# Attention scores from float32r halves on two row tiles, with the maxima of two heads taken in one reduce

## The chip, the cores and the metric

The kernel runs on one core of one Trainium2 chip. Its time is what the device took for one execution, in microseconds (us). Of several runs the median is given; one further execution was profiled, and all rows of engines, waits and chains below come from that one.

## The reference

One sequence of 2048 tokens with 256 features goes through six stages, each added to the residual x after a layer norm: feed-forward f0, attention 0, feed-forward f1 (the same weights as f0), feed-forward f2 (another kind), attention 1, feed-forward f3 (as f2). Cut to the two attentions, which the change concerns:

```python
qkv = x @ W_qkv                       # layer 1: x @ Wq.T + bq, and so on, then rope on q and k
q, k, v = heads(qkv)                  # 16 heads of 16 features
attn = q @ k.T / 4 + alibi + causal   # layer 1: no alibi; alibi = slope[head] * (j - i)
attn = softmax(attn)
y = attn @ v
x = x + y @ W_o                       # layer 1: + bo
```

Everything is float32. In layer 1 the biases of q and k are large, so the scores need more than the precision of one bf16 product.

## The kernel before

The sequence is cut into four chunks of 512 columns (`CH`), and features lie on the partitions. The feed-forwards go chunk by chunk (`feed_forwards`, line 457): gate and up products in float32r pairs (f0, f1: `gate_up0`, line 295, each activation split into a top part and a rest) or in float32 (f2, f3: `gate_up`, line 271), an activation, a projection back (`tail0`, `tail1`). In f0 the weights are quantized beside the first chunk (`quantize`, line 130), from raw tiles that SP loads. The attentions are one function (`attention`, line 513), called for each layer.

**Scores from parts.** `prep_qk` (line 544) makes q and k of one chunk, splits each value into three bf16 parts (cast on ACT, differences on DVE and POOL) and writes them to DRAM so that six products of parts (`Q_PARTS`, `K_PARTS`) lie under each other. `load` (line 651) reads, for a group `n` of four heads and a chunk, tiles `qs[n]` and `ks[n, kc]`: 96 rows of six products by 16 features, and below them rows for the negated row maximum (three bf16 parts) and, in layer 0, for the alibi bias. One bf16 matmul over these 105 rows (99 in layer 1) gives the scores of one head for 128 x 512 places, with the maximum already subtracted once its rows are there.

**Two passes.** The score is taken twice. `mx_unit` (line 702) computes it with the queries on the partitions (tile `pq`, one PSUM bank for each head) and reduces it on DVE to the maximum of each row (line 721). When all maxima of a group are there, `mx_end` and `mx_turn` negate, split and transpose them and put them into the rows of `qs[n]` by DMA. Then `st_pair` (line 764) computes the transposed scores of two heads (tile `pst`, two banks), `exp_pair` takes their exponential on ACT into `pT` (one instruction for two heads, line 792; of the pairs in slots without a unit every third lies in two single banks, line 795), and `av_part` (line 798) multiplies by v: four heads at once on four column tiles of 32 columns, all into one bank `pav`, in float32. A column of ones in v gives the sum of the exponentials; `divide` (line 818) transposes and divides.

**Diagonal blocks.** Where keys and queries are of the same chunk, a further bf16 matmul of 128 columns adds a causal mask for each head (lines 718 and 780).

**Order.** PE, ACT, DVE and POOL run in the order in which the program is written; SP's DMAs are ordered by the framework. The main loop (line 985) goes over 160 slots in each layer: slot (n, kb) is a group of four heads (16 of them, four for each chunk of queries) and a block of 128 keys. A slot takes two `st_pair`s, the units of maxima planned for it (`maxima`, one in most slots, two in 12, none in 19, for a group that comes later), two `exp_pair`s, the pav of an earlier slot (`sums`), and then one step of the preparation of the next chunk, of the output projection, of a layer norm or of `mx_turn`. In a slot with a unit the four heads of the unit stand two by two behind the two `st_pair`s. If the slot is the first, the second or one of the last five of its group, pav is taken in two pieces, one behind each pair; otherwise in one, at the end.

**PSUM.** There are three pools for the whole kernel (lines 55 to 57): two tiles of two banks (`pair`), three of one bank (`one`) and one of one bank (`acc`). `pst` lies in `pair`; `pq` lies in `one`, as do all smaller products in attention (`pp`, `pv`, `pwo`, `ptm`, layer norms); `pav` is `acc`.

Of the kernel before, what the change touches and what calls it, by code (L numbers as in the profile page):

```python
# [12 lines left out]
F32 = mybir.dt.float32  # L13
BF16 = mybir.dt.bfloat16
# [24 lines left out]
Q_PARTS = (0, 0, 1, 1, 0, 2)  # L39
K_PARTS = (0, 1, 0, 1, 2, 0)  # L40
TERMS = len(Q_PARTS)
RM = TERMS * D
ROWS = {0: RM + 9, 1: RM + 3}
# [4 lines left out]
def macaron_kernel(ctx: ExitStack, tc: tile.TileContext, a, out):  # L48
# [6 lines left out]
    ps2 = ctx.enter_context(tc.tile_pool(name="ps2", bufs=2, space=PSUM))  # L55
    ps3 = ctx.enter_context(tc.tile_pool(name="ps3", bufs=3, space=PSUM))
    ps1 = ctx.enter_context(tc.tile_pool(name="ps1", bufs=1, space=PSUM))

    def ps_pair(name):
        return ps2.tile([P, 2, CH], F32, tag="pair", name=name)  # L60

    def ps_one(name):
        return ps3.tile([P, CH], F32, tag="one", name=name)

    def ps_acc(name):
        return ps1.tile([P, CH], F32, tag="acc", name=name)
# [22 lines left out]
    ident = cpool.tile([P, P], F32, name="ident")  # L89
    make_identity(nc, ident)  # L90
    ident_b = cpool.tile([P, P], BF16, name="ident_b")
    nc.vector.tensor_copy(ident_b, ident)

    mask_qk = cpool.tile([P, P], BF16, name="mask_qk")
    mask_kq = cpool.tile([P, P], BF16, name="mask_kq")
    for mask, step, row in ((mask_qk, -1, 1), (mask_kq, 1, -1)):
        nc.gpsimd.memset(mask, 0.0)
        nc.gpsimd.affine_select(
            out=mask, in_=mask, compare_op=ALU.is_ge, fill=MASK, base=0, pattern=[[step, P]],
            channel_multiplier=row,  # L100
        )

    half_m = cpool.tile([P, P], BF16, name="half_m")
    nc.vector.memset(half_m, 0.0)
    nc.vector.memset(half_m[0:64, 0:64], 1.0)
    nc.vector.memset(half_m[64:128, 64:128], 1.0)
# [3 lines left out]
    ones_m = cpool.tile([P, P], F32, name="ones_m")  # L110
    nc.vector.memset(ones_m, 1.0)
# [6 lines left out]
    lpool = ctx.enter_context(tc.tile_pool(name="ln", bufs=1))  # L118
# [9 lines left out]
    qp = raw_scope.enter_context(tc.tile_pool(name="quant", bufs=3, side="right"))  # L128
# [220 lines left out]
    def tail0(c, ss, parts, hp, own, name):  # L349
# [23 lines left out]
        nc.tensor.matmul(pss, lhsT=ones_m, rhs=ss, start=True, stop=True)  # L373
        r = root(pss, eps_rms, 4.0 / F, f"rms_{name}")
# [138 lines left out]
    def attention(layer, before, following):  # L513
# [9 lines left out]
        with ExitStack() as st:  # L523
# [5 lines left out]
                for w in "kq"  # L529
                for c in range(NCH)  # L530
            }

            def values(pool, c):
# [692 lines left out]
```

## Time and profile before

| | |
|---|---|
| median of 3 runs | 1827.77 us (1824.9 to 1831.12) |
| profiled execution: its time | 1831.77 us |
| profiled execution: its span, from the first to the last instruction | 1830.0 us |
| mean granted TensorE clock | 0.974 |
| attention of layer 0, by its stages | 212 to 756 us |
| attention of layer 1, by its stages | 1085 to 1647 us |
| HBM read, written | 59.51 MB, 27.26 MB |

In the profile PE is TensorE's matmuls, PEld its weight loads, DVE is VectorE, ACT ScalarE, POOL GpSimd and SP the engine that issues most DMAs. A row of the timeline gives start, length, engine, line, operation, what it writes and reads, the shape and the number of instructions joined in it; in brackets stand the idle time of the engine just before it and what ended that. Rows joined run from the start of the first to the end of the last, and ends of matmuls are modelled, so the spacing of starts tells more than the length. A row of stages gives the stretch, its length, and busy time and number of instructions for PE, PEld, DVE, ACT and POOL, then the granted clock, the share of the DMA engines and GB/s.

### The profile page before, as it was taken

The page shows a single profiled execution, that of the slowest core. Times are in us where ns is not written, and L with a number is a line of the kernel's source. Part 1 is how long each engine was busy: PE and PEld are TensorE (multiplying, and loading weights), DVE is VectorE, ACT ScalarE, POOL GpSimd, SP SyncE. Part 2 cuts the span into 40 slices and gives each one's busy share as a digit, 9 for nine tenths or more (in the row PEclk, how much of TensorE's full clock was granted, in tenths as well). Part 3 has the DMA queues.
Part 4 walks back from the last instruction along what each step waited for, and adds up shares of the span by engine and source line. Part 5 has one row for each costly group of instructions (what it writes and reads, how often), then busy time and mean ns, then how long its engine had stood idle before and what let it go on. Part 6 is the DMA issues. An engine that isn't in the chain of part 4 may idle for free.

```text
span 1830.0 us, 26213 instructions
## 1 busy us (share of the span) xinstructions
PE 1648.4 (90%) x10299; PEld 782.5 (43%) x10300; DVE 1314.3 (72%) x2368; ACT 911.8 (50%) x1220; POOL 347.0 (19%) x346
## 2 busy tenths in 40 slices
PE   4498888999999999788899998899999999988999
PEld 2365543444434443366444444334434434433443
DVE  7865687787788884466666677778788888816664
ACT  4365354555565667555423325445565556674221
POOL 3355520200000001265411232122001000012000
PEclk9799899999999999999999999999999999999999
DMA  4003332212211110200000334222122110000000
GB/s 138 2 1 105 114 95 79 72 54 76 93 41 47 30 30 1 78 1 1 13 0 1 103 109 130 66 85 90 48 65 90 46 46 28 11 2 0 12 12 23
DMA packets 50508, 93.06 MB, mean 51 GB/s; under 512 B 5424, under 2 KB 33072, under 8 KB 50128
## 3 DMA queue, kind: packets, MB, share of 16 engines
q1 hardware_dynamic: 49296, 89.28, 15.9%
q10 hardware_dynamic: 1088, 2.10, 0.4%
q8 instruction: 81, 1.33, 0.3%
q14 instruction: 43, 0.35, 0.1%
HBM read 59.51 MB, written 27.26 MB: 47 GB/s over the span
## 4 chain that ended last, share of the span: by engine, by line
PE 62%; DVE 19%; ACT 4%; issue 2%; POOL 2%; DMA 1%; SPq 0%; DVEq 0%; ACTq 0%; POOLq 0%
PE pav L807 14%; PE pst L772 12%; PE pq L710 11%; DVE mx L721 8%; PE pg_f L276 7%; PE po_f L287 5%; PE pg_f L301 2%; PE pwo L848 2%; PE pp_k L557 2%; PE pp_q L557 1%; PE po_f L356 1%; DVE ge_f L408 1%; PE pv L622 1%; PE pst L780 1%; PE pq L718 1%
## 5 line engine op out<-in xcount | busy, mean ns | idle before, releaser
L721 DVE TENSOR_REDUCE mx<-pq 128x1 f32<-128x512 f32 (+3 forms) x1280 | 696.7, 602 | 132.8 <-PE pq L718 65.4
L792 ACT ACTIVATE pT<-pst 128x1024 f32<-128x1024 f32 (+3 forms) x616 | 536.2, 897 | 335.8 <-PE pst L772 170.7
L710 PE MATMUL pq<-k,q 105*128 105x512 bf16 (+7 forms) x1280 | 385.9, 349 | 53.2 <-DVE mx L721 46.4
L772 PE MATMUL pst<-q,k 99*128 99x512 bf16 (+7 forms) x1280 | 356.5, 352 | 10.6 <-ACT pT L792 6.7
L807 PE MATMUL pav<-pT,va 128*32 128x256 f32 (+1 forms) x4608 | 324.7, 377 | 6.2 <-DVE yt L828 5.0
L276 PE MATMUL pg_f<-xn,wgu 128*128 128x512 f32 x512 | 230.5, 602 | 15.0 <-DVE hr_f L314 15.0
L772 PEld LDWEIGHTS <-k 105*128 105x128 bf16 (+1 forms) x1280 | 111.5, 98 | 233.7 <-issue 168.3
L833 POOL TENSOR_TENSOR zt<-yt,rd 128x64 f32<-128x64 f32 x128 | 42.1, 329 | 807.3 <-DVE rd L832 803.0
L807 PEld LDWEIGHTS pav<-pT,va 128*32 128x32 f32 x4608 | 106.3, 108 | 191.5 <-issue 136.8
L710 PEld LDWEIGHTS <-q 105*128 105x128 bf16 (+1 forms) x1280 | 122.9, 98 | 128.9 <-issue 26.5
L313 ACT ACTIVATE sl_f<-pg_f 128x512 f32<-128x512 f32 x128 | 75.9, 593 | 174.7 <-PE pg_f L276 98.3
L276 PEld LDWEIGHTS pg_f<-xn,wgu 128*128 128x128 f32 x512 | 97.4, 192 | 142.8 <-issue 115.1
L301 PE MATMUL pg_f<-xt_f,wgu 128*128 128x512 f32 x256 | 101.0, 478 | 37.8 <-DVE sl_f L314 20.9
L287 PE MATMUL po_f<-h_f,wd 128*128 128x512 f32 x256 | 112.6, 593 | 1.4 <-DVE h_f L436 1.4
L718 PE MATMUL pq<-mask_qk,ident_b 128*128 128x128 bf16 x512 | 105.4, 222 | 0.0
L780 PE MATMUL pst<-mask_kq,ident_b 128*128 128x128 bf16 x512 | 103.1, 221 | 0.0
L334 POOL TENSOR_TENSOR ss_f<-ss_f,sq_f 128x512 f32<-128x512 f32 x56 | 85.2, 1521 | 88.8 <-ACT sq_f L333 88.2
L314 DVE TENSOR_TENSOR hr_f<-sl_f,pg_f 128x512 f32<-128x512 f32 x64 | 43.7, 683 | 69.1 <-ACT sl_f L313 68.8
L828 DVE STREAM_TRANSPOSE yt<-pav 128x128 f32<-128x128 f32 x128 | 39.8, 311 | 71.1 <-PE pav L807 71.1
L301 PE MATMUL pg_f<-xr_f,wgu 128*128 128x512 f32 x256 | 86.0, 419 | 1.5 <-DVE xr_f L231 1.5
L314 DVE TENSOR_TENSOR sl_f<-sl_f,pg_f 128x512 f32<-128x512 f32 x64 | 43.7, 682 | 60.2 <-ACT sl_f L313 59.8
L301 PEld LDWEIGHTS pg_f<-xt_f,wgu 128*128 128x128 f32 x256 | 51.7, 208 | 80.8 <-DVE sl_f L314 27.5
(134 smaller groups left out, 1755.1 us busy)
## 6 DMA issues: line engine op xcount, KB each, us to landing
k<-dk SPq DMA_DIRECT2D x80, 384.0 KB
dk<-p_k SPq DMA_DIRECT2D x48, 256.0 KB
dq<-p_q SPq DMA_DIRECT2D x48, 256.0 KB
q<-dq SPq DMA_DIRECT2D x32, 384.0 KB
x<-in_xT ACTq DMA_DIRECT2D x4, 512.0 KB
raw<-in_w_gu SPq DMA_DIRECT2D x8, 256.0 KB
wgu<-in_w_gu SPq DMA_DIRECT2D x1, 2048.0 KB
cs_k<-in_cos_sin SPq DMA_DIRECT2D x4, 512.0 KB
```

What stands on the lines that cost most here:

```text
L276: nc.tensor.matmul(pg[:, half, :], lhsT=wgu[:, dc, half * F + f * P : half * F + (f + 1) * P], rhs=xn[:, dc, :], start=dc == 0, stop=dc == ...
L287: nc.tensor.matmul(po, lhsT=w[:, f, dc * P : (dc + 1) * P], rhs=h[:, f, :], start=f == 0, stop=f == FC - 1,)
L301: nc.tensor.matmul(pg[:, half, :], lhsT=wgu0[:, dc, half * F + f * P : half * F + (f + 1) * P], rhs=xp[part][:, dc, :], start=part == 0 an ...
L314: nc.vector.tensor_tensor(to, sl, pg[:, 1, :], ALU.mult)
L334: nc.gpsimd.tensor_tensor(ss, ss, sq, ALU.add)
L710: nc.tensor.matmul(pq, lhsT=qs[n][0:rows, hh, t * P : (t + 1) * P], rhs=ks[n, kc][0:rows, hh, 0:w], start=True, stop=kc < c,)
L718: nc.tensor.matmul(pq[:, w - P : w], lhsT=ident_b, rhs=mask_qk, start=False, stop=True)
L721: nc.vector.tensor_reduce(mxs[n][:, t, hh, kc : kc + 1], pq, AX.X, ALU.max)
L772: nc.tensor.matmul(ps[i][:, lo:CH], lhsT=ks[n, kc][0:rows, hh, t * P : (t + 1) * P], rhs=qs[n][0:rows, hh, lo:CH], start=True, stop=kc < c,)
L780: nc.tensor.matmul(ps[i][:, lo : lo + P], lhsT=ident_b, rhs=mask_kq, start=False, stop=True)
L792: nc.scalar.activation(pT[:, :, lo:CH], pair[:, :, lo:CH], AF.Exp, scale=0.25)
L807: nc.tensor.matmul(acc[hh * SLOT : (hh + 1) * SLOT, a:b], lhsT=va[kc][:, t, v0 : v0 + SLOT], rhs=pTs[hh // 2][:, hh % 2, a:b], start=kb == ...
```

## The change

- **Parts.** q and k are split into two float32r parts instead of three bf16 parts (top, and the rest by one subtraction that writes float32r), and three products are kept instead of six. The 52 rows of a head (48 and 4; layer 1: 50) fit into 64 partitions, so two heads lie under each other, at partitions 0 and 64, and the four heads of a group in two columns. The bytes of the tiles and of the DRAM parts stay; a load is four DMAs instead of two.
- **Scores.** `score` issues the matmuls of two heads one behind the other, one on each row tile of 64 rows, into two banks, and the mask, where there is one, as two halves of 64 rows for each head (`eye`, and masks cut in two). Both passes use it.
- **Maxima.** `pq` is a tile of two banks, and one reduce takes the maxima of two heads. The maxima are split into two float32r parts, and go to `qs[n]` in four DMAs instead of three.
- **PSUM.** During attention the pools are three `pair`, one `one`, one `acc`; outside it they are as before.
- **Slots.** pav is taken in one piece at the end of every slot, exp follows each pair, and no pair lies in single banks.
- **Constants.** The rows of biases go through one load, a cast on DVE and a write to DRAM at the start; the masks are made on POOL after the first layer norm; `ones_m` is dropped; three tags of the quantizer have two buffers instead of three. In the order in which SP issues, the load of wqkv (768 KB) now stands ahead of the raw weights.

```diff
-Q_PARTS = (0, 0, 1, 1, 0, 2)
-K_PARTS = (0, 1, 0, 1, 2, 0)
+Q_PARTS = (0, 0, 1)
+K_PARTS = (0, 1, 0)
 TERMS = len(Q_PARTS)
 RM = TERMS * D
-ROWS = {0: RM + 9, 1: RM + 3}
+ROWS = {0: RM + 4, 1: RM + 2}
+HALF = P // 2
...
+    def halves(t, step, row, compare, fill):
+        nc.gpsimd.memset(t, 0.0)
+        for b in range(2):
+            for j in range(2):
+                at = t[b * HALF : (b + 1) * HALF, j, :]
+                nc.gpsimd.affine_select(
+                    out=at, in_=at, compare_op=compare, fill=fill, base=row * j * HALF,
+                    pattern=[[step, P]], channel_multiplier=row,
+                )
+
+    def make_masks():
+        halves(eye, -1, 1, ALU.not_equal, 1.0)
+        halves(mask_qk, -1, 1, ALU.is_ge, MASK)
+        halves(mask_kq, 1, -1, ALU.is_ge, MASK)
...
                     if layer == 0:
                         nc.scalar.copy(pt[0][:, i, :], pp)
-                        nc.vector.tensor_tensor(dn[:, i, :], pp, pt[0][:, i, :], ALU.subtract)
+                        nc.vector.tensor_tensor(
+                            pt[1][:, i, :], pp, pt[0][:, i, :].bitcast(F32), ALU.subtract
+                        )
...
-                    nc.vector.tensor_tensor(dn, dn, pt[0], ALU.subtract)
+                    nc.vector.tensor_tensor(pt[1], dn, pt[0].bitcast(F32), ALU.subtract)
                 yield
-                nc.scalar.copy(pt[1], dn)
-                nc.gpsimd.tensor_tensor(pt[2], dn, pt[1], ALU.subtract)
-                yield
-                for j in range(3):
+                for j in range(2):
...
                 def stack(to, what, of, extra):
+                    halves = to.bitcast(F32).rearrange("(b r) a t -> b r a t", b=2)
+                    for b in range(2):
+                        u = g % 2 * 4 + 2 * b
+                        nc.sync.dma_start(
+                            out=halves[b, 0:RM],
+                            in_=parts[what, of][g // 2]
+                            .bitcast(F32)
+                            .rearrange("m (d u) t -> (m d) u t", u=HB)[:, u : u + 2, :],
+                        )
+                        nc.sync.dma_start(
+                            out=halves[b, RM:rows], in_=extra[b, 0 : rows - RM].bitcast(F32)
+                        )
...
             pools.insert(0, kv)
+            open_psum(3, 1)
...
-            def mx_unit(n, t, kc, heads):
+            def score(out, lhsT, rhs, mask, at):
+
+                for b in range(2):
+                    nc.tensor.matmul(
+                        out[:, b, :], lhsT=lhsT[b * HALF : b * HALF + rows],
+                        rhs=rhs[b * HALF : b * HALF + rows], start=True, stop=mask is None,
+                    )
+                if mask is not None:
+                    for j in range(2):
+                        for b in range(2):
+                            h = slice(b * HALF, (b + 1) * HALF)
+                            nc.tensor.matmul(
+                                out[:, b, at : at + P], lhsT=eye[h, j, :], rhs=mask[h, j, :],
+                                start=False, stop=j == 1,
+                            )
+
+            def mx_unit(n, t, kc, pair):
...
-                for hh in heads:
-                    pq = ps_one(f"pq{layer}_{n}_{t}_{kc}_{hh}")[:, 0:w]
...
-                    nc.vector.tensor_reduce(mxs[n][:, t, hh, kc : kc + 1], pq, AX.X, ALU.max)
+                pq = ps_pair(f"pq{layer}_{n}_{t}_{kc}_{pair}")[:, :, 0:w]
+                score(
+                    pq,
+                    qs[n][:, pair, t * P : (t + 1) * P],
+                    ks[n, kc][:, pair, 0:w],
+                    mask_qk if kc == c else None,
+                    w - P,
+                )
+                nc.vector.tensor_reduce(mxs[n][:, t, pair::2, kc], pq, AX.X, ALU.max)
...
-                for m in range(3):
-                    nc.sync.dma_start(out=qs[n][RM + m : RM + m + 1, :, :], in_=qx[4 * m : 4 * m + 4, :])
+                for m in range(2):
+                    for b in range(2):
+                        at = b * HALF + RM + m
+                        nc.sync.dma_start(
+                            out=qs[n].bitcast(F32)[at : at + 1, :, :],
+                            in_=qx.bitcast(F32)[4 * m + 2 * b : 4 * m + 2 * b + 2, :],
+                        )
...
-                if units:
-
-
-                    full = 1 < kb < c * T - 1
-                    for hp in (1, 0):
-                        ps = st_pair(n, kb, hp)
-                        mx_next(units[0], (2 - 2 * hp, 3 - 2 * hp))
-                        pTs[hp] = exp_pair(n, kb, hp, ps)
-                        if not full:
-                            sums(i - 2 + (hp == 0), hp)
-                    if full:
-                        sums(i - 1, 1)
-                else:
...
+                for pair in (1, 0):
+                    ps = st_pair(n, kb, pair)
+                    if units:
+                        mx_next(units[0], (pair,))
+                    pTs[pair] = exp_pair(n, kb, pair, ps)
+                sums(i - 1, 1)
...
     load_x(0, nc.scalar)
+    raw = rp.tile([P, CH], F32, tag="raw", name="raw_bias")
+    nc.scalar.dma_start(out=raw, in_=a["bias"])
+    bias = lpool.tile([P, CH], F32R, tag="sd", bufs=2, name="bias")
+    nc.vector.tensor_copy(bias, raw)
+    biases = dram.tile([2, NCH, 2, 4, 2, CH], F32R, name="biases")
+    nc.sync.dma_start(
+        out=biases.bitcast(F32).rearrange("w n b r a t -> (w n b r a) t"), in_=bias.bitcast(F32)
+    )
```

## Prediction

> **What bounds the kernel now.** I read the page first, for the engines and the chain that ended last.
>
> ```profile
> PE 1648.4 (90%) x10299; PEld 782.5 (43%) x10300; DVE 1314.3 (72%) x2368; ACT 911.8 (50%) x1220; POOL 347.0 (19%) x346
> ...
> PE 62%; DVE 19%; ACT 4%; issue 2%; POOL 2%; DMA 1%; SPq 0%; DVEq 0%; ACTq 0%; POOLq 0%
> ```
>
> PE is the chain. The busy times by stage show where the edited lines stand: attention of layer 0 runs from 212 to 756 us, of layer 1 from 1085 to 1647 us.
>
> ```profile
> 572.00:747.00 175.00, 169.60 (x1506) 68.67 (x1505) 119.22 (x227) 118.22 (x143) 9.63 (x20) 1.00 0.08 24
> ```
>
> In the last chunk of layer 0 PE (first figure after the length) is busy 169.6 of 175 us, DVE 119, ACT 118. Third, the timeline of one interior slot with a maxima unit:
>
> ```profile
> 644.83 0.61 PE L772 MATMUL pst<-q,k 105*128 105x512 bf16 x2
> 645.05 0.31 PEld L710 LDWEIGHTS <-q 105*128 105x128 bf16 x2
> 645.27 0.59 PE L710 MATMUL pq<-k,q 105*128 105x512 bf16 x2
> 645.47 1.95 ACT L792 ACTIVATE pT<-pst 128x1024 f32<-128x1024 f32 x2 [0.96 <-PE pst L772]
> 645.49 0.31 PEld L772 LDWEIGHTS <-k 105*128 105x128 bf16 x2
> 645.68 2.49 DVE L721 TENSOR_REDUCE mx<-pq 128x1 f32<-128x512 f32 x4 [0.43 <-PE pq L710]
> 645.70 0.59 PE L772 MATMUL pst<-q,k 105*128 105x512 bf16 x2
> 645.92 0.31 PEld L710 LDWEIGHTS <-q 105*128 105x128 bf16 x2
> 646.13 0.67 PE L710 MATMUL pq<-k,q 105*128 105x512 bf16 x2
> 646.73 0.59 PEld L807 LDWEIGHTS pav<-pT,va 128*32 128x32 f32 x16 [0.50 <-issue]
> 646.74 1.07 PE L807 MATMUL pav<-pT,va 128*32 128x256 f32 x16
> 647.73 0.11 PEld L772 LDWEIGHTS <-k 105*128 105x128 bf16 x2 [0.41 <-issue]
> 647.74 0.39 PE L772 MATMUL pst<-q,k 105*128 105x512 bf16 x1
> ```
>
> A slot is 647.74 - 644.83 = 2.91 us of PE without a hole: eight score matmuls 0.216 apart, then pav. DVE needs 2.49 of it, ACT 1.95. Taking each slot's first pst row, the medians are: interior 2.91 (pav in one piece), 3.02 (in two), 4.63 (two units), 1.97 (no unit); diagonal slots with a unit, by width 512, 384, 256, 128: 3.55, 3.34, 2.60, 2.18.
>
> **The score matmuls.** Two float32r matmuls of 52 (layer 1: 50) rows on two row tiles take the place of two bf16 ones. What float32r costs stands in the feed-forward, where one (L301) waited for DVE (sl_f):
>
> ```profile
> 764.83 0.69 DVE L314 TENSOR_TENSOR sl_f<-sl_f,pg_f 128x512 f32<-128x512 f32 x1 [2.30 <-ACT sl_f L313]
> ...
> 765.57 0.30 PEld L301 LDWEIGHTS pg_f<-xt_f,wgu 128*128 128x128 f32 x2 [2.52 <-DVE sl_f L314]
> 765.57 0.73 PE L301 MATMUL pg_f<-xt_f,wgu 128*128 128x512 f32 x2 [2.10 <-DVE sl_f L314]
> ...
> 765.91 0.42 PEld L301 LDWEIGHTS pg_f<-xr_f,wgu 128*128 128x128 f32 x2
> ```
>
> In a stream they are 0.23 us apart, nearly the bf16 spacing. But here the weight load itself waits, begins 0.052 after DVE ends (765.517), and the first of the two matmuls takes 0.34 instead of 0.23: 0.108 of the load is exposed. The bf16 load at 645.92/646.13 runs ahead of its matmul's wait, and the first pst after pav pays only 0.01. Four-byte loads after pav (pwo, pp) also expose 0.107. Two row tiles at once are in no row; nearest are the column tiles of pav: four matmuls 7 ns apart, whose 16 loads take 0.59 together, like the groups of four, 0.216 apart. So a pair costs between one matmul (0.23) and two (0.46); I take 0.23, the loads likewise side by side.
>
> The page "TensorE: Matmul & The Clock Gate" of the Trainium skill, "Weight-path perf modes", speaks against the change: fast weight load is only for 128 columns that are not FP32. The rows agree for float32r (exposed 0.108 against 0.01), and a sum that loads float32r as fast as bf16 would make the slot 0.2 shorter than mine. Its Part 3 gives 3.07 times for four row tiles, not 4; an estimate from that page puts a pair at about 0.28 instead of 0.23, some 0.1 us more per slot; no run here shows it.
>
> **PSUM is what ends last then.** pst and pq now share three two-bank buffers. A slot uses four: st of pair 1, max of pair 1, st of pair 0, max of pair 0; the fourth takes the buffer of the first and waits for exp of pair 1, in PE's own order, with the whole pav and the next slot's st queued behind it. That closes a loop:
>
> - exp of 1024: 1.025 (L792 by form); release to load: 0.052; exposed load: 0.108
> - max matmuls to first pav: 0.306 (646.429 to 646.735); pav to the next st load: 0.999 (to 647.734)
> - exposed load again 0.108, then pst to exp 0.415 (645.053 to 645.468)
>
> Sum 3.01 us, against 2.91 now. PE would idle some 0.8 us in each slot, and the halved score work lands there. DVE stays below: a reduce costs 281, 417, 549, 682 ns at 128, 256, 384, 512, so 1024 costs 1.217, two 2.43. Merging saves little of DVE: neighbours overlap by 0.08 now (four in 2.49).
>
> By slot kind, per layer (160 slots):
>
> - 51 interior with pav in one piece: 2.91 to 3.01, +5
> - 25 interior with pav in two: one piece now, two tile changes (about 0.09 each way) saved, 3.02 to 3.01, 0; 8 with two units: four reduces, 4 x 1.13, bind as now, 4.6, 0
> - 12 without unit: ACT binds, 2 x 0.925 = 1.85 against 1.97, -1
> - 53 diagonal with one unit: the same loop with exp 1.025, 0.811, 0.593, 0.383, with the slot's own masks (four half-height ones in two steps of 0.06) and the pav of the slot before (0.999, 0.999, 0.78, 0.57): 3.20, 2.88, 2.33, 1.90. 15 x -0.35, 12 x -0.46, 13 x -0.27, 13 x -0.28 = -18
> - 11 other diagonal slots, about -0.3 each: -3
>
> That is -17 per layer, -34 in all.
>
> **What goes the other way.** (1) Other PE work in the slots (pp, pv, pwo, layer norm, ptm; about 45 groups a layer) stands after pav and before the next st, so it lengthens the loop as it lengthens PE now; but the float32r load after it is exposed: 90 x 0.1 = +9. (2) All of it shares one bank instead of three: at 15 places in the order two such groups stand in one slot, and the second waits for an eviction of 0.6 to 1.2 us: +10 (bounds 0 and 18). (3) At the start, SP now issues the 768 KB load of wqkv ahead of the raw weights. The first raw landed at 4.3 us and DVE's chain starts from it, 79% busy in the first slice; at the 380 to 400 KB/us that the DMA moved from 9 to 13 us, 768 KB are 2 us, and the cast of the bias rows on DVE 0.7: +3 (bounds 0 and 5).
>
> **What costs or gains nothing.** The preparation of q and k loses a cast on ACT (1.04 us, 16 times) and a subtraction on POOL (2.16, 16 times). Both stand beside FFN or attention PE work, but at 155.9 the POOL one runs while DVE's hl_f takes 2.52 instead of 0.68 and PE waits 2.01 for it: -3 in all (bounds 0 and -8). DMA bytes are the same; SP issues 671 rows instead of 456, 215 x 0.4 = 86 us of issue spread over 1100, ahead of need by three slots, hidden; if the cover goes, a late k costs about 2 us each time. The q rows of the maxima take four DMAs instead of three: 0.4 behind a 1.7 us landing, at the four places where the chain shows one: within 2 us. POOL's mask selects (12 x 0.29) fall into POOL's idle 23.3 to 25.2 and before x of chunk 1 is needed.
>
> Sum: -34 + 9 + 10 + 3 - 3 = -15. The profiled execution took 1831.8, the median of the runs is 4 less: 1817, and 1813 for the median.
>
> **Rivals.**
>
> - *The loads of the two tiles follow each other.* Then each exposed place of the loop costs 0.108 more: 141 slots with a unit x 0.22 x 2 layers = +61, 1874: slower. For it: each float32r load blocks the next for 0.108 (765.57 to 765.68). Against it: pav's loads of four tiles overlap. It decides as soon as the interior slot is over 3.1 us. Chance 0.16.
> - *The tiles don't run at once* (the change doesn't do what it says): a pair costs 0.46, both pairs in the loop 0.22 more, masks too: 141 x 0.43 x 2 = +121, 1934. Chance 0.07.
> - *PE's clock falls.* The second slice, PE 49% busy, ran at 0.75 clock; the slots would have PE streaming (0.86 + 0.86) / 3.01 = 57%. A slot at half clock adds about 1.5 us; one in ten makes 32 x 1.5 = +48, 1861. Chance 0.1.
> - *The loop is looser*: loads run ahead of the waits as bf16's do, 0.108 twice per slot off: -61, 1752. Against it: the wait of PEld at 765.57. Chance 0.12.
>
> **Numbers.** The forecast case, 1813, has 0.55; its own terms (each slot known to some 0.1 us over 300 slots) make it 1785 to 1845. About 0.3% (5.5 us) is what a measurement of this kernel can tell from no change; within the case I give 0.65 to faster by more, 0.18 to within, 0.17 to slower. Faster: 0.55 x 0.65 + 0.12 = 0.48; within: 0.10; slower: 0.42. The range 1752 to 1880 takes in the looser loop and the serial loads, and leaves out the case of no concurrency and the worse half of a fallen clock.
>
> **What would show it.** Right: interior slots at 3.0 us, PE's idle before the max matmuls of pair 0 put down to ACT (exp), two score matmuls starting within 10 ns; diagonal slots shorter by 0.3; DVE rows of 1.2 us. Wrong: score pairs 0.3 or more apart (serial loads) or 0.45 (no concurrency); PEclk below 9 in the attention slices; interior slots at 2.8 (loads ahead); or waits of PE on DVE instead of ACT, which would make the reduce the bound.

## The result, and the profile after

The changed kernel takes 1953.76 us (median of 4 runs, 1938.03 to 1968.75) against 1829.44 for the kernel before: a ratio of 1.0653, 95% interval 1.0564 to 1.0742. It is slower, and the forecast was 1813. The ratio is that of the mean times of the fast runs (the run of 1968.75 counts as slow and is left out, a fifth run of 1950.65 is taken in), so it is below the quotient of the medians. The profiled execution took 1966.04, the longest of the four that the ratio takes in, at the lowest granted clock of them (0.899; the others 0.904 to 0.920); its span is 1964.1. First the page: the rows of busy time, of the chain, and of the granted clock in 40 slices.

```profile
PE 1645.9 (84%) x11324; PEld 819.9 (42%) x11324; DVE 1288.9 (66%) x1728; ACT 889.3 (45%) x1180; POOL 317.4 (16%) x341
...
PEclk9799757779988899998999996699898799999999
...
PE 54%; ACT 15%; DVE 14%; issue 4%; POOL 2%; DMA 1%; SPq 0%; DVEq 0%; ACTq 0%; POOLq 0%
```

PE is busy as long as before (1645.9 against 1648.4) in a longer span; ACT's share of the chain went from 4% to 15%; and the clock, 9 in most slices before, is at 5 to 7 in the first slices of the first attention (a slice is 49 us) and at 6 in the first two of the second. Cut from the first slot of each attention to its last, the stages read so (length; busy time of PE, PEld, DVE, ACT, POOL; granted clock):

```profile
224.87:823.82 598.95, 504.05 (x4658) 235.72 (x4658) 382.70 (x510) 299.38 (x362) 34.35 (x75) 0.84 0.18 49
1185.77:1772.98 587.21, 488.91 (x4680) 231.70 (x4677) 399.90 (x529) 303.53 (x360) 51.23 (x85) 0.89 0.21 55
```

Before, they took 519.00 and 537.49 us at clocks of 0.99 and 0.98. So 130 of the span's 134 us more are lost here. The start, where I had expected 3 us more, is within the scatter of the runs: attention begins at 224.9 (before 227.9; in the kernels below 222 to 232).

**The interior slot is as forecast.** The same timeline as before, one interior slot with a maxima unit:

```profile
701.40 0.50 PE L741 MATMUL pst<-q,k 52*128 52x512 f32 x2
701.51 0.19 PEld L741 LDWEIGHTS pq<-k,q 52*128 52x128 f32 x2
701.74 0.40 PE L741 MATMUL pq<-k,q 52*128 52x512 f32 x2
701.80 0.19 PEld L741 LDWEIGHTS pst<-q,k 52*128 52x128 f32 x2
701.94 1.94 ACT L828 ACTIVATE pT<-pst 128x1024 f32<-128x1024 f32 x2 [1.11 <-PE pst L741]
701.97 0.39 PE L741 MATMUL pst<-q,k 52*128 52x512 f32 x2
...
703.02 0.50 PE L741 MATMUL pq<-k,q 52*128 52x512 f32 x2 [0.66 <-ACT pT L828]
...
703.45 1.07 PE L840 MATMUL pav<-pT,va 128*32 128x256 f32 x16
...
704.45 0.50 PE L741 MATMUL pst<-q,k 52*128 52x512 f32 x2
```

Two score matmuls share one row (x2): they and their weight loads start 3 or 4 ns apart, and the next pair follows 0.23 later (701.74 to 701.97). The fourth use of the three buffers, pq at 703.02, waits for ACT's exp with pav behind it. The loop: exp and release 701.94 to 703.02, 1.08; to pav 0.43; pav to the next scores 1.00; those to exp 0.54; together 3.05.

**The diagonal slot is not.** One whose unit is 384 wide (the first row is the maxima of pair 1):

```profile
683.31 0.96 DVE L768 TENSOR_REDUCE mx<-pq 128x2 f32<-128x768 f32 x1
...
684.32 0.64 PE L840 MATMUL pav<-pT,va 128*32 128x256 f32 x8
684.43 0.96 DVE L768 TENSOR_REDUCE mx<-pq 128x2 f32<-128x768 f32 x1 [0.16 <-PE pq L749]
685.30 0.30 DVE L861 STREAM_TRANSPOSE yt<-pav 128x128 f32<-128x128 f32 x1
...
685.66 0.64 PE L840 MATMUL pav<-pT,va 128*32 128x256 f32 x8 [0.71 <-DVE yt L861]
```

pav has two parts, and `av_part` calls `divide` between them: yt transposes the finished columns of the same bank. Here the first part ends while DVE is in the second reduce of 0.96; yt starts when that is done, and only after yt the second part of pav. Before, the scores of the other pair stood between the parts. This slot takes 4.23 us where 2.88 was forecast. (0.34 of it is `ptm`, which half of the slots of this width hold, before the change too, and which the 2.88 leaves out.)

**The clock is the third thing.** Three windows of 3.4 us (columns as in the stages above):

```profile
426.40:429.80 3.40, 2.72 (x40) 1.56 (x38) 2.33 (x5) 1.96 (x4) 0.29 (x1) 1.00 0.45 124
429.80:433.20 3.40, 1.98 (x18) 0.81 (x18) 3.19 (x6) 1.77 (x2) 0.29 (x1) 1.00 0.55 131
433.20:436.70 3.50, 3.50 (x22) 1.22 (x22) 3.19 (x3) 1.02 (x1) 0.00 (x0) 0.51 0.00 0
```

After a window with PE busy 1.98 of 3.40 and DVE 3.19, PE runs at half clock. What stands in that window isn't a diagonal slot but the end of an interior slot with two units, and the slot after it:

```profile
430.46 0.74 PE L741 MATMUL pq<-k,q 52*128 52x512 f32 x4
...
431.50 0.50 PE L741 MATMUL pst<-q,k 52*128 52x512 f32 x2 [0.30 <-DVE mx L768]
...
431.80 4.59 DVE L768 TENSOR_REDUCE mx<-pq 128x2 f32<-128x1024 f32 x4
...
433.12 0.71 PE L741 MATMUL pq<-k,q 52*128 52x512 f32 x2 [1.12 <-ACT pT L828]
```

PE issues the second unit's maxima at once (430.46) and goes on. DVE then has four reduces in a row (4.59 us), the second unit's two and the next slot's own. The next scores wait for a buffer from DVE (0.30), the next maxima for exp (1.12). Of the 16 interior slots with two units in both layers 15 have half clock in them or in the slot behind them (2 of 16 before). All stretches of half clock in the trace are multiples of 3.41 us long; in the two attentions there are 21, from 3.4 to 65 us, and they add up to 319 us (25 before). An interior slot that lies in one takes 4.50.

### The profile page after: what moved, and what is told of

The parts are those of the page before. It is cut to its first block, busy times and chain, and to the rows that moved or that the text cites. A ratio compares the mean times of both kernels' runs of the same rounds, so it can differ in the third digit from the quotient of the medians.

```text
span 1964.1 us, 27868 instructions
## 1 busy us (share of the span) xinstructions
PE 1645.9 (84%) x11324; PEld 819.9 (42%) x11324; DVE 1288.9 (66%) x1728; ACT 889.3 (45%) x1180; POOL 317.4 (16%) x341
## 4 chain that ended last, share of the span: by engine, by line
PE 54%; ACT 15%; DVE 14%; issue 4%; POOL 2%; DMA 1%; SPq 0%; DVEq 0%; ACTq 0%; POOLq 0%
PE pav L840 14%; ACT pT L828 12%; PE pq L741 9%; PE pst L741 7%; PE pg_f L298 6%; PE po_f L309 5%; DVE mx L768 5%; PE pg_f L323 2%; PE pp_k L584 2%; PE pq L749 1%; PE pwo L881 1%; PE pv L651 1%; PE po_f L378 1%; PE pst L749 1%; DVE ge_f L430 1%
## 5 line engine op out<-in xcount | busy, mean ns | idle before, releaser
L768 DVE TENSOR_REDUCE mx<-pq 128x2 f32<-128x1024 f32 (+3 forms) x640 | 671.6, 1062 | 245.9 <-PE pq L749 127.7
L741 PE MATMUL pq<-k,q 52*128 52x512 f32 (+7 forms) x1280 | 309.0, 483 | 132.0 <-ACT pT L828 114.2
L840 PE MATMUL pav<-pT,va 128*32 128x256 f32 (+1 forms) x4608 | 357.2, 417 | 42.5 <-DVE yt L861 40.1
L741 PE MATMUL pst<-q,k 50*128 50x512 f32 (+7 forms) x1280 | 304.1, 472 | 13.0 <-DVE mx L768 7.6
L741 PEld LDWEIGHTS pq<-k,q 52*128 52x128 f32 (+1 forms) x1280 | 137.9, 213 | 242.5 <-ACT pT L828 201.0
L741 PEld LDWEIGHTS pst<-q,k 52*128 52x128 f32 (+1 forms) x1280 | 135.6, 208 | 182.3 <-issue 115.2
L840 PEld LDWEIGHTS pav<-pT,va 128*32 128x32 f32 x4608 | 117.9, 116 | 190.0 <-DVE yt L861 70.7
L749 PEld LDWEIGHTS <-eye 64*128 64x128 bf16 x2048 | 68.3, 107 | 48.5 <-issue 28.6
L749 PE MATMUL pq<-mask_qk,eye 64*128 64x128 bf16 x1024 | 85.0, 248 | 0.0
L749 PE MATMUL pst<-mask_kq,eye 64*128 64x128 bf16 x1024 | 83.0, 243 | 0.0
```

What stands on the lines that cost most here:

```text
L741: nc.tensor.matmul(out[:, b, :], lhsT=lhsT[b * HALF : b * HALF + rows], rhs=rhs[b * HALF : b * HALF + rows], start=True, stop=mask is None,)
L749: nc.tensor.matmul(out[:, b, at : at + P], lhsT=eye[h, j, :], rhs=mask[h, j, :], start=False, stop=j == 1,)
L768: nc.vector.tensor_reduce(mxs[n][:, t, pair::2, kc], pq, AX.X, ALU.max)
L840: nc.tensor.matmul(acc[hh * SLOT : (hh + 1) * SLOT, a:b], lhsT=va[kc][:, t, v0 : v0 + SLOT], rhs=pTs[hh % 2][:, hh // 2, a:b], start=kb == ...
```

## The experiments

Slot times are medians over both layers at full clock, as in the prediction; diagonal ones for unit widths 512, 384, 256, 128. "Half clock" is the time at half clock, and "attention" the length, of the two attention stages, in each profiled execution.

| kernel | interior | diagonal | half clock | attention | median | ratio to before (95%) |
|---|---|---|---|---|---|---|
| before | 2.91, 3.02 | 3.55 3.34 2.60 2.18 | 25 | 1056 | 1829.4 | |
| changed | 3.05 | 3.31 4.23 3.21 1.89 | 319 | 1186 | 1953.8 | 1.0653 (1.0564 to 1.0742) |
| e1 | 3.05 | 3.31 3.31 2.46 1.89 | 246 | 1119 | 1903.3 | 1.0368 (1.0332 to 1.0403) |
| e2 | 3.05 | 3.10 3.19 2.54 2.29 | 268 | 1124 | 1902.7 | 1.0387 (1.0366 to 1.0408) |
| e3 | 2.68 | 3.12 3.18 2.52 2.29 | 360 | 1115 | 1884.8 | 1.0296 (1.0257 to 1.0335) |
| e4 | 2.95 | 3.09 3.41 2.53 2.34 | 332 | 1159 | 1938.9 | 1.0583 (1.0543 to 1.0623) |
| e5 | 3.05 | 3.5 4.66 3.58 2.16 | 66 | 1162 | 1956.1 | 1.0674 (1.0640 to 1.0708) |
| e6 | 3.05 | 3.5 3.60 2.82 2.16 | 60 | 1107 | 1897.0 | 1.0360 (1.0308 to 1.0412) |
| e7 | 2.99 | 3.6 3.66 3.00 2.65 | 376 | 1223 | 1994.6 | 1.0886 (1.0818 to 1.0955) |
| e8 | 3.24 | 3.48 4.17 3.19 1.77 | 39 | 1141 | 1914.2 | 1.0446 (1.0416 to 1.0476) |
| e9 | 2.68 | 3.12 3.27 2.55 2.29 | 140 | 1043 | 1828.6 | 0.9974 (0.9951 to 0.9997) |
| e10 | 3.05 | 3.31 4.22 3.21 1.89 | 201 | 1156 | 1946.0 | 1.0613 (1.0589 to 1.0637) |
| e11 | 3.08 | 3.56 3.34 2.60 2.22 | 10 | 1065 | 1840.7 | 1.0053 (1.0037 to 1.0070) |
| e12 | 2.68 | 3.12 3.27 2.54 2.29 | 80 | 1029 | 1808.2 | 0.9862 (0.9838 to 0.9886) |

The theory when the first runs were made: the wait for yt is the first cause, and the falls of the clock follow from the idle PE that it makes. The rival: the clock falls whatever waits in the diagonal slots.

**e1: yt after both parts of pav.**

```diff
-                if part == 0 and kc == c:
+                if part == 1 and kc == c:
                     divide(n, t)
```

> The changed kernel with one edit: in a diagonal slot the transpose of the accumulator on DVE (yt) is issued after the second part of pav and not between the two parts, so that the second part no longer waits for it. Nothing of the work is left out. Theory A (the wait of pav for yt, queued on DVE behind the second maximum of 0.96 us, is the first cause; the falls of the clock follow from the idle PE that it makes): the second diagonal slot goes from 4.23 to about 2.9 us, the third from 3.21 to about 2.3, the interior slot stays at 3.05; 12 x 1.35 + 13 x 0.88 = 28 us per layer, 56 in all at full clock, and of the 319 us of attention that PE spends at half clock (worth some 100 us) most go too: 1810 to 1850 us. Rival B (the clock falls because of the loop of the interior slots or because two 52-row tiles count as less activity than one of 105 rows, whatever waits in the diagonal slots): the half clock stays above 250 us in the attention stages, and only the 56 us go: about 1900.

The time is B's, and the half clock nearly (246 against above 250). The slots answered as A says, though less: 3.31 and 2.46, where A had about 2.9 and 2.3 (without `ptm` the first is 2.98), and pav stands in one row with yt behind it:

```profile
647.98 1.07 PE L840 MATMUL pav<-pT,va 128*32 128x256 f32 x16
648.09 0.96 DVE L768 TENSOR_REDUCE mx<-pq 128x2 f32<-128x768 f32 x1 [0.16 <-PE pq L749]
...
649.12 0.32 DVE L861 STREAM_TRANSPOSE yt<-pav 128x128 f32<-128x128 f32 x1
```

The time fell by 50 us, of which the slots give 24 x 0.92 + 26 x 0.75 = 42 for the two widths. But the half clock only fell to 246, in 23 stretches, so the wait for yt is a cause of its own and not what most of the falls follow from.

**e2 and e3: the parts of pav apart**, in slots outside the interior (e2, as before the change) or in every slot with a unit (e3):

```diff
                     pTs[pair] = exp_pair(n, kb, pair, ps)
-                sums(i - 1, 1)
+                    if units and not 1 < kb < c * T - 1:   # e3: if units:
+                        sums(i - 2 + (pair == 0), pair)
+                if not units or 1 < kb < c * T - 1:        # e3: if not units:
+                    sums(i - 1, 1)
```

> The changed kernel with the place of pav as in the kernel before: in slots that are not interior its two parts stand apart, one after the maxima of each pair (which also frees PE's order from the wait for exp there), in interior slots in one piece. Nothing of the work is left out. Theory A (the lost distance between the parts of pav is what cost): yt is hidden behind the scores of the second pair again; diagonal slots at 3.0, 2.5, 2.1, 1.8, shorter than the loop's 3.20, 2.88, 2.33, 1.90 since pav now fills the wait for exp; interior stays 3.05; half clock below 100 us; 1790 to 1830. Rival B (clock falls come from the row tiles or the interior loop): half clock above 250 us, about 1890.

> As the run with parts of pav apart in the diagonal slots, but apart in every slot with a unit, the interior ones too: the order is scores, maxima, part of pav, scores, maxima, part of pav. Nothing of the work is left out. Theory A (in the interior slot the maxima of the second pair wait for exp of the first with the whole pav queued behind them): half of pav now runs inside that wait, and the loop is shorter by about 0.5 us: DVE with its two reduces of 1.226 becomes the bound at 2.5 to 2.6 us; 76 x 2 x 0.45 = 68 us less than with the parts apart in diagonal slots only: 1725 to 1770, faster than the kernel before. Rival C (the interior slot is bound by exposed weight loads and pair times on PE, not by the wait): interior stays at 2.95 to 3.05, within 10 us of the run with parts apart in the diagonal slots.

The place of the parts answers for the interior slot as theory A said and rival C did not: with half of pav inside the wait for exp it takes 2.68, near DVE's two reduces of 1.23. In time both missed A's ranges by some 70 us and more, with 268 and 360 us at half clock; e2's time and half clock are near rival B's. Theory A for the clock had fallen.

**e4: the row tiles alone**, maxima again in single banks with four reduces, PSUM as before:

```diff
-                pq = ps_pair(f"pq{layer}_{n}_{t}_{kc}_{pair}")[:, :, 0:w]
+                pq = [ps_one(f"pq{layer}_{n}_{t}_{kc}_{pair}_{b}")[:, 0:w] for b in range(2)]
...
-                nc.vector.tensor_reduce(mxs[n][:, t, pair::2, kc], pq, AX.X, ALU.max)
+                for b in range(2):
+                    hh = pair + 2 * b
+                    nc.vector.tensor_reduce(mxs[n][:, t, hh, kc : kc + 1], pq[b], AX.X, ALU.max)
```

> The float32r row tiles alone: maxima again in four single banks with one reduce per head, PSUM again two pairs and three single banks, the place of pav as in the kernel before (as in the run with parts apart in the diagonal slots). Nothing of the work is left out. Theory A (the loop comes from sharing three two-bank buffers between scores and maxima; the row tiles themselves are a gain): no maxima wait for exp; DVE's four reduces of about 0.68 (2.5 to 2.75 us) bind the interior slot at 2.5 to 2.75; 76 x 2 x 0.4 = 60 us less than the same order with merged maxima: 1730 to 1790. Rival D (float32r pairs with their exposed loads are what ends last): interior at 2.95 or more, 1800 or more.

A miss for A, and D's number for another reason than D's:

```profile
739.93 2.48 DVE L769 TENSOR_REDUCE mx<-pq 128x1 f32<-128x512 f32 x4 [0.47 <-PE pq L740]
...
740.67 0.50 PE L740 MATMUL pq<-k,q 52*128 52x512 f32 x1 [0.31 <-DVE mx L769]
741.10 1.07 PE L841 MATMUL pav<-pT,va 128*32 128x256 f32 x16
```

No load ends last: the fourth of four maxima waits for one of three single banks, for DVE, and pav stands behind it again. Three buffers for four uses make a loop either way; only the releaser changes.

**A rule for the clock.** I cut the traces into the windows of 3.41 us in which the clock changes, and took in each the time in which PE streams: 0.216 us for the 512 columns of a score matmul (the spacing in a bf16 stream) and for the 256 columns of one of pav's, twice that at half clock, each times its rows in use out of 128, four column tiles of pav counted as one. Take the windows of these six profiles that hold only scores and pav. Some 1040 are at full clock, and the clock falls after about 100 of them: they part at 0.36 (below it the clock falls), with 8 to 15 on the wrong side, depending on where, within 0.3 us, the edges of the windows are set. Some 335 are at half clock, and it comes back after 60: they part at 0.75 (above it the clock comes back), with 26 to 44 wrong, so this second edge is rough. An interior slot, then, doesn't make the clock fall, but by itself hardly brings it back: at full clock four pairs of 0.216 x 104/128 and pav of 0.86 are 1.57 of 3.05, or 0.51; at half clock twice that, 3.13, of 4.50, or 0.70. The rule was found by looking at these traces, so the next runs were to test it, against the rival that waits alone or float32r itself set the clock.

**e5, e6, e7: a filler**, bf16 matmuls whose result is overwritten, ahead of the maxima of pair 1: four of them in the changed kernel (e5) and in e1's (e6), two in e3's (e7).

```diff
                 pq = ps_pair(f"pq{layer}_{n}_{t}_{kc}_{pair}")[:, :, 0:w]
+                for _ in range(2 if pair == 1 else 0):   # e7: 1
+                    for b in range(2):
+                        nc.tensor.matmul(
+                            pq[:, b, 0 : min(w, 256)], lhsT=eye[:, 0, :],
+                            rhs=mask_qk.rearrange("p j t -> p (j t)")[:, 0 : min(w, 256)],
+                            start=True, stop=True,
+                        )
```

> The changed kernel, with work added that no result needs: ahead of each maxima pair 1, four bf16 matmuls of 128 rows and 256 columns (0.43 us at full clock) into the same bank, which the real ones then overwrite. They stand where PE idles about 0.8 us for exp. Theory E (in the traces so far the clock fell after a 3.4 us window in which PE streamed less than 0.36 of the time, weighted by rows in use, and came back after one above 0.75; the slots with two row tiles reach only 0.69 at half clock, so they stay there): with the filler a slot at half clock reaches about 0.85 and comes back after one or two windows; half clock in the attention stages falls from 319 us to under 80, worth some 80 us, interior slots stay at 3.05 and the waits for yt stay: 1860 to 1890, with more work done. Rival F (the falls are set by the waits alone, or by float32r itself): half clock stays above 200 us and the time is 1950 or more.

> Both edits: the transpose of the accumulator issued after the second part of pav, and the filler of 0.43 us ahead of the first maxima of a slot. Theory E: half clock under 50 us, interior 3.05, diagonal slots 3.3, 3.3, 2.5, 1.9: 1810 to 1845 us, which is what my prediction's loop gives (1813). Rival F: half clock stays near the 246 us of the run without filler, 1890 or more.

> Parts of pav apart in every slot with a unit, and a filler of two matmuls (0.21 us) ahead of the first maxima of a slot. Theory E: half clock from 322 us to under 100, interior 2.7 to 2.85 at full clock: 1770 to 1820, faster than the kernel before, though PE does more. Rival F: half clock stays above 250, 1880 or more.

The half clock did what the rule said in e5 and e6 (319 to 66, 246 to 60), the interior slot stayed at 3.05, and the time hardly moved: it is 66 and 52 us above E's ranges, and where F had it. The filler lengthens the diagonal slots by 0.2 to 0.4 and takes most of what the clock gives. With each slot at the full-clock median of its kind, the attentions of the changed kernel come to 967 us and of e5 to 1006; what is above that in the profiled executions, 219 and 156, holds the half clock: so what the filler removed of it was worth some 63 us, of which the filler took 39 (for e1 and e6: 50 and 39). e7 missed: here the filler isn't hidden (2.99), and at half clock the slot grew to 5.16. The rule, had I worked it out for that slot, gives (3.13 + 0.43) / 5.16 = 0.69, no better than without: 376 us at half.

**e8 and e11: the ring without row tiles**, bf16 scores as before, maxima in pairs from the three shared buffers; pav in one piece at the end (e8) or its parts apart in every slot with a unit (e11).

```diff
-                for hh in heads:
-                    pq = ps_one(f"pq{layer}_{n}_{t}_{kc}_{hh}")[:, 0:w]
+                h0 = heads[0]
+                pq = ps_pair(f"pq{layer}_{n}_{t}_{kc}_{h0}")[:, :, 0:w]
+                for b, hh in enumerate(heads):
...
-                    nc.vector.tensor_reduce(mxs[n][:, t, hh, kc : kc + 1], pq, AX.X, ALU.max)
+                nc.vector.tensor_reduce(mxs[n][:, t, h0 : h0 + 2, kc], pq, AX.X, ALU.max)
```

> The kernel before with only the other half of the change: bf16 scores of all 105 rows, one head at a time, but maxima of two heads by one reduce over two banks, three two-bank buffers shared by scores and maxima, one single bank, and both parts of pav at the end of the slot. Nothing of the work is left out. Theory A+E (the ring and the place of pav cost by themselves, the row tiles are what lets the clock fall): interior slots at 3.2 (the same loop with one more bf16 matmul, 0.216, at each of two places), second and third diagonal slots above 4 and 3.4 with the wait for yt, half clock under 60 us, 1890 to 1940. Rival F (the waits alone make the clock fall): half clock over 200 us, 1980 or more. Rival G (the ring costs nothing, the row tiles do): 1840 or less.

> The kernel before with bf16 scores of 105 rows, maxima of two heads by one reduce, three two-bank buffers shared, one single bank, and the two parts of pav apart in every slot with a unit: against the run with 64-row tiles it differs by the row tiles alone. Nothing of the work is left out. Theory A+E: the loop is about 2.73 us (exp 1.025, release 0.05, two maxima 0.52, half of pav 0.5, two scores to exp 0.63), under PE's own 8 x 0.216 + pav in two parts, so PE binds the interior slot at 2.9 to 3.0; two-unit slots fall to about 3.6; half clock under 50 us: 1805 to 1840. The row tiles then give 0.25 us in each of 152 interior slots, some 38 us, and the half clock takes most of it back: the two runs within 25 us of each other. Rival I (the row tiles are worth their face value): 1860 or more, against 1828 for the run with 64-row tiles.

e8 is theory A and E nearly to the number: 3.24, 4.17, 3.19 (3.4 expected), 1914 us, 39 us of half clock. So the ring and the place of pav cost 82 us without any row tile, and the same waits nearly leave the clock alone when PE streams 105 rows for twice as long. The changed kernel, with the row tiles besides, is by the ratios some 38 us slower still. e11's interior slot is 0.1 longer than expected (3.08) and its time just above the upper end (1840.7).

**e9 and e10: the row tiles padded to 64 rows** with zeros, in e3's order (e9) and in the changed kernel (e10). Nothing else changes: the result, the waits and the length of the matmuls are the same, and a load of q or k has one DMA more for each half (HBM read in e9 71.7 MB, in the changed kernel 59.8).

```diff
-                        out[:, b, :], lhsT=lhsT[b * HALF : b * HALF + rows],
-                        rhs=rhs[b * HALF : b * HALF + rows], start=True, stop=mask is None,
+                        out[:, b, :], lhsT=lhsT[b * HALF : (b + 1) * HALF],
+                        rhs=rhs[b * HALF : (b + 1) * HALF], start=True, stop=mask is None,
...
+                        nc.sync.dma_start(
+                            out=halves[b, rows:HALF], in_=zeros[0 : HALF - rows]
+                        )
```

> Parts of pav apart in every slot with a unit, without filler, and the two row tiles padded with rows of zeros from 52 (50) to 64 rows, loaded by one more DMA for each half of q and k; the result is the same, the matmuls take as long and PE waits in the same places. Theory E (the clock follows the streaming time weighted by rows in use): over the half-clock windows of the run without padding, the share that passes 0.75 goes from 12% to 66% when the pairs count as 64 rows, and 5 of 17 falls are avoided; half clock goes from 322 us to 100 to 150, worth 60 to 90 us: 1790 to 1830, at or under the kernel before. Rival H (rows in use do not count, only whether PE streams): half clock stays at 280 to 350 us, 1880 to 1900.

> The changed kernel with only the padding to 64 rows. Theory E: 20% of the half-clock windows of the changed kernel passed 0.75, 50% would with 64 rows, and 7 of 19 falls are avoided; half clock from 319 us to 130 to 180, worth 30 to 45 us; the waits for yt (4.23 and 3.21) stay: 1905 to 1930. Rival H: half clock 280 to 350 us, 1945 to 1965.

Rows of zeros make the kernel faster in e3's order: e9 takes 56 us less than e3 with nearly the same slot medians, and half clock falls from 360 us (the expectation has 322, an addition of mine that was wrong) to 140. The granted clock of the whole execution agrees in every run: 0.882 to 0.895 in e3, 0.933 to 0.941 in e9. Rival H is out there. The clock falls as often (20 and 21 stretches), but a stretch lasts 6 us instead of 17 in the mean: the padding brings the clock back sooner and hardly keeps it from falling. Most of the falls of e9 come, as in the changed kernel, in the slot after one with two units, where DVE is behind. In e10 the profiled execution has 201 us of half clock, between the two expectations and nearer to E's, but the time is where H had put it (1946.0). Here the two profiled executions mislead: the changed kernel's has the lowest clock of its runs (0.899 against 0.904 to 0.920), and e10's runs lie at 0.914 to 0.923. Since the clock in the traces is either full or half, twice what is missing to 1, times the span, is the time at half clock of the whole execution: some 350 us in the mean over the changed kernel's runs, some 310 in e10, where e3 and e9 have some 418 and 230. So most of the difference of 118 us in the table isn't the padding's, and e10's time shows no gain that is clear of the scatter. Why the padding does so little in this order stays open.

Between e11 and e9 stand the row tiles and their padding, at the same place of pav; but e11 is made from the kernel before, so the split into two float32r parts, the halved masks, the loads and the order of slots without a unit differ as well. With all slots at their full-clock medians the attentions take 948 and 865 us, a gain of 83; as measured 1065 and 1043. The clock and the slots with other work take 62 back.

**e12: e9 with a filler in one place**, ahead of the first scores of a slot that follows one with two units:

```diff
-                    ps = st_pair(n, kb, pair)
+                    ps = st_pair(n, kb, pair, 2 * (pair == 1 and len(maxima.get(i - 1, [])) > 1))
```

> The run with 64-row tiles and the parts of pav apart, with a filler of four bf16 matmuls (0.43 us) in one place only: ahead of the first scores of a slot that follows a slot with two maxima units, where DVE is 4.6 us behind and PE idles over 1 us for it. Theory E: 16 of the 23 falls of the clock in the attention stages of the 64-row run came after a window of 0.22 to 0.33 that holds such a slot; with 0.43 / 3.41 = 0.13 more most of these stay above 0.36; half clock in attention from 140 to under 70 us, at some 2 us a fall 20 to 32 us less: 1795 to 1812, faster than the kernel before beyond doubt. Rival J (the idle is on the path, and the filler only lengthens it by 16 x 0.43 = 7): 1828 to 1840.

1808.19 us (5 runs, 1802.07 to 1813.22), ratio 0.9862, 95% interval 0.9838 to 0.9886: the only version clearly faster than the kernel before (1.4%), inside E's range and outside J's. Half clock is 80 us (E had under 70), in 12 stretches where e9 has 21. The stage of layer 0 in e5, e9 and e12:

```profile
232.25:805.91 573.66, 522.63 (x5275) 256.96 (x5270) 375.44 (x511) 308.78 (x362) 34.30 (x75) 0.98 0.19 50
```

```profile
228.45:743.90 515.45, 473.18 (x4662) 212.30 (x4658) 379.41 (x511) 307.16 (x362) 34.31 (x75) 0.94 0.24 67
```

```profile
223.27:733.25 509.98, 473.12 (x4707) 214.94 (x4707) 378.16 (x509) 307.77 (x362) 34.44 (x75) 0.96 0.24 68
```

The clock alone doesn't rank them: e5 has the best (0.98) and the longest stage. It keeps the changed kernel's order, with the wait for yt, and its filler keeps PE busy for nothing (522.63). The order of work and the clock together do.

## Why the prediction was wrong

- **The loop of the interior slots: right.** 3.01 forecast, 3.05 measured, each term within 0.02. The waits, the pairs at 0.23, the loads side by side and the reduce of 1.23 (1.217) are as it said.
- **The diagonal slots: the step that failed first.** The prediction took "the pav of the slot before (0.999, 0.999, 0.78, 0.57)" as one stretch, and counted one piece in place of two as a saving. But the second part waits for yt, and yt on DVE for the reduce of the last maxima. Forecast 3.20, 2.88, 2.33, 1.90; measured 3.31, 4.23, 3.21, 1.89; without that wait (e1) 3.31, 3.31, 2.46, 1.89. It cost some 50 us. What is left at the second width is mostly `ptm`: without it these slots of e1 take 2.98. The forecast set a slot without `ptm` against a median that holds it (before: 3.13 without, 3.33 with), so the saving of 0.46 was too large as well.
- **The clock: the larger cost, held for a rival with a tenth of the chance, and with too narrow a condition.** The prediction weighed 57% of streaming in an interior slot against one slice of the trace, and had nothing on how a clock that has fallen comes back, nor on rows in use. Most falls (12 of 21) came in or behind a slot with two units, and the interior slots hardly ended them. Its 48 us were too low for the profiled execution. The 63 and 50 by e5 and e6 are lower bounds, since these still spend 66 and 60 us at half clock. Slot by slot, 77 slots of the changed kernel touch half clock; 61 of them have slots of the same kind, with the same other work, at full clock, and take 92 us more than those; the other 16 have none to compare with. The page "TensorE: Matmul & The Clock Gate" of the Trainium skill has a section "A second HAM failure mode: psum-queue depth-cycling", which tells of a kernel whose PE idles briefly between groups of matmuls while PSUM banks go round, and whose clock swings between half and full; this trace agrees (319 us at half), and the prediction should have weighed it.
- **Two-unit slots: where most of the falls began.** 4.6 forecast, "bind as now", at no cost; 3.47 measured. But this is no gain: PE leaves the slot while DVE still has reduces to do, and they run over into the next slot (the 4.59 us shown above). That slot takes 5.27 in the median instead of 3.05, half clock included, and the two together 8.9 against 7.7 before. In e5, with the filler, they take 8.0 at full clock; in e12, 7.3. The test is e12's filler, which stands in these places alone: 12 stretches of half clock instead of e9's 21, and 20 us less.
- **What the rest came to.** 1817 forecast in the profiled frame, some 50 for yt and at least 92 for the clock make about 1960 of 1966. This is an estimate: the 16 slots without a match, and smaller terms of both signs, are not taken apart. Of the single bank for other PE work one place can be read: three interior slots at full clock that hold both `pp` and `pwo` take 7.79 in the median, where slots with one of the two take 4.99 and with none 3.05; 7.79 - 3.05 - 2 x 1.94 leaves 0.86 that the second costs more, which over the prediction's 15 places would be 13 us, near its 10. No run tested it apart.
- **The range** left out the case that happened: the prediction had no rival for the wait on yt, and it says itself that the range leaves out the worse half of a fallen clock. Both came, and together.

## What to carry to other kernels

When an engine gets faster, look for what it now waits for in its own order: with three buffers for four uses the fast engine stands at the fourth, and everything behind it stands too, so put independent work (here half of pav) between the uses. When a slot comes out shorter than forecast, look at the one behind it: it may hold the work that was put off. Before pieces of work are put together, look at what is called between them and at the queue of the engine that must do it. And in this case a TensorE that idled and used fewer rows lost its clock: work out the streaming share, by rows, of the slot at half clock too, since here that went with how soon the clock came back. Compare clocks over all runs, and not from one profile of each kernel.

## What the runs showed of the hardware

- Two float32r matmuls of 52 rows on two row tiles start 3 or 4 ns apart and the next pair 0.233 later, for 0.432 that two bf16 ones of 105 rows took: the two run at once, and so do their weight loads. (The estimate of 0.28 that the prediction made from Part 3 of the page "TensorE: Matmul & The Clock Gate" of the Trainium skill was too high.)
- The clock fell after windows of 3.41 us with a weighted streaming share under 0.36 and mostly came back after one above 0.75 (over the ten profiles up to e8, 14 to 26 of some 1890 windows at full clock are on the wrong side, where 130 end in a fall, and 33 to 57 of some 450 at half clock, where 78 end in a return). In e12 a few falls came at 0.37 to 0.39, so 0.36 is no sharp edge either. The window's length agrees with the 3413 ns that the same page states in its Part 1; its "abstract rule" of no idle gaps above some 3.4 us (section "HAM oscillation — how this bites in real kernels") is not enough here: in the window shown (429.8 to 433.2) PE's longest gap between matmuls was 1.12 us, and the clock fell after it.
- Rows of zeros count as rows in use: with padding from 52 to 64 rows and parts of pav apart, half clock went from 360 to 140 us (e3 to e9), in as many but shorter stretches. In the changed kernel's order (e10) the runs show little of it.
